# A two-layer graph kernel: guarded parts without SyncE's DMAs, gates ahead of the branch, layer two's weights in another order

## The chip, the cores and the metric

One core of a Trainium2 chip runs the whole kernel. TensorE (PE) multiplies, VectorE (DVE), ScalarE (ACT) and GpSimd (POOL) do the rest, SyncE (SP) issues most of the loads. The metric is the device time of one launch in microseconds (us); the lower, the better.

## The reference, cut to what matters

625 nodes with 512 features, 20,625 edges (10,000 in both directions and the loops), float32. Two layers. Layer 0, where the change lies, is a relational graph network of two inner layers, a linear attention, and a mixture of experts:

```python
def rgcn_gate_layer(x, row, col, edge_type, basis, att, gate_w, root, bias):
    w = jnp.einsum('rb,bio->rio', att, basis)          # 2 relations from 30 bases of 512 x 512
    x_j = x[col]
    msgs = [jax.nn.sigmoid(x_j @ gate_w[r, :, 0])[:, None] * x_j @ w[r] for r in range(2)]
    msg = jnp.where((edge_type == 0)[:, None], msgs[0], msgs[1])
    return jax.ops.segment_sum(msg, row, num_segments=625) + x @ root + bias

h = relu(rgcn_gate_layer(xn, ..., basis1, att1, gate_w1, root1, bias1))
gnn = rgcn_gate_layer(h, ..., basis2, att2, gate_w2, root2, bias2)
x = x + gnn + linear_attention(xn) @ W_out + b_out
x = x + one_of_8_experts(layernorm(x))
```

Layer 1 (a graph attention network, another attention, two of eight experts) fills the second half of the time and is not touched.

## The kernel before

The nodes are held as five tiles of 125. Nothing is gathered by edge: the kernel first counts, for each relation and each pair of nodes, the edges between them. One field of a float32 holds five nodes tiles and both relations in two bits each (`count_group`, `decode_fields`), ten tiles `counts` of 125 x 626. Messages are then a dense product of the counts with what each node sends. Should a pair have more edges than two bits hold, the fields are wrong; a sum over all of them, compared with the number of edges, gives a `flag`, and four guarded parts (`with tc.If(again > 0)`, L530, L580 twice, L806) do the exact work: `count_any` counts in a loop and stores the exact counts in DRAM (`cexact`, `cover`), `over` adds products to open PSUM banks, and the last one reloads counts. With these inputs the flag is 0, and every guarded part is skipped. Each engine that has something in a guarded part passes its branch, and where it has DMAs there, it has to keep their semaphores in step on the skipped way.

The weights `w` of each relation, a sum over 30 bases, are made while the data streams in. There are two ways to do it:
- a **P step** (`Bases.product`, L330) does it on TensorE for 32 of the 512 input rows in two steps, 15 bases each. Its load is four DMAs of 240 KB on SyncE's queue (`rows_of`, L321). After each second one ScalarE copies the result (L334), and GpSimd sends it to its rows of `wmix` with four DMAs (L337);
- a **D step** (`Bases.add`, L355) does it on VectorE for one basis and 384 of the 512 rows: two instructions of 128 x 1536, one for each relation. Its load is one DMA of 768 KB (`basis`, L342).

Layer one's weights are all made by P steps (`mix`), behind the counting. Layer two's need 8 P steps (rows 0 to 127) and 30 D steps (rows 128 to 511). `PLAN` gives their order, `second("DDP")` puts the next steps of the plan at a place in the program, and `load_next` asks for the next load after each. All loads of bases share a pool of three buffers; load n waits for the step that used its buffer last, and it is queued on SyncE behind load n-1 and whatever else stands before it (`root`, `root2`, `wout`: 1 MB each, through `load_w`).

TensorE, VectorE and SyncE run this part in the order in which the program states it (`manual_schedule`). That order is: the last counts are decoded; head sums of the attention (`key_value_sums`) with the last `mix` products between; the flag; the branch at L530; gates of layer one (`gate_sums`: products, a copy on ScalarE, a second product, a sigmoid in `gates_of`) with a P step between; the attention's values for five tiles (`mixed_values`) with two D steps and a P step; `messages(1)`: ten groups of 8 matmuls, each followed by a step or two of the plan; bias rows; the branch of `over`; then for each of five tiles the root product, transposes, 20 products with the counts (`summed`) and two D steps; own products of layer two (`own_pairs`, root and attention's output) with more D steps; all that is left of the plan; `messages(2)` (line L139, 80 matmuls), its branch, and layer two's sums. `five_banks` gives five PSUM banks for the tiles: two pairs and a single one, taken in order. Further on, `loops_added` (L789) adds up the counts for layer 1 on GpSimd behind the last guarded part, while the experts' products run.

Of the kernel before, what the change touches and what calls it, by code (L numbers as in the profile page):

```python
# [8 lines left out]
F32 = mybir.dt.float32  # L9
F32R = mybir.dt.float32r  # L10
# [9 lines left out]
P = 125  # L20
NT = 5
# [3 lines left out]
ODG = 11  # L25
NW = 626
NB = 30
PLAN = "PDDPDPDDPDPDDPDDPDP" + 19 * "D"
BGROUPS = (15, 15)
BROWS = 8  # L30
EXTRA = 4
# [6 lines left out]
def cols(t):  # L38
    return slice(t * P, (t + 1) * P)
# [7 lines left out]
def kernel(ctx: ExitStack, tc: tile.TileContext, A, out: bass.AP):  # L47
# [123 lines left out]
    def one_bank():  # L171
        return banks[1].tile([128, BANK], F32, name="ps1")
# [85 lines left out]
        return flag  # L258

    cexact = tc.dram_tile([2 * NT, P, NW], F32, name="cexact")  # L260
    cover = tc.dram_tile([2 * NT, P, NW], F32, name="cover")

    def count_any():

        held = [w8.tile([128, KD * D], F32, tag="w", name="whole") for _ in range(3)]
        whole = [held[i // 3][:P, NW * (i % 3):NW * (i % 3) + NW] for i in range(9)]
        whole.append(dec.tile([P, NW], F32, tag="vf", name="whole9"))
        for c in whole:  # L270
            nc.gpsimd.memset(c, 0.0)
        with tc.For_i(0, NE, 1) as c:
            some = dec.tile([P, 3], I32, name="some")
            for i, n in enumerate(("src", "dst", "edge_type_2")):
                nc.sync.dma_start(some[:, i:i + 1], A[n].rearrange("(p c) -> p c", p=P)[:, bass.ds(c, 1)])
            ends = dec.tile([P, 3 + NT], F32, name="some_f")
            nc.vector.tensor_copy(ends[:, 0:1], some[:, 0:1])
            nc.vector.tensor_scalar(ends[:, 2:3], some[:, 2:3], 0.0, None, op0=OP.not_equal)
            nc.vector.tensor_scalar(ends[:, 1:2], some[:, 2:3], 0.0, None, op0=OP.is_equal)
            for t in range(NT):  # L280
                nc.vector.tensor_scalar(ends[:, 3 + t:4 + t], some[:, 1:2], -float(t * P), None, op0=OP.add)
            os_ = [ohp.tile([P, NW], BF, name="os") for _ in range(2)]
            for r in range(2):
                nc.vector.tensor_scalar(os_[r], iota, ends[:, 0:1], ends[:, 1 + r:2 + r],
                                        op0=OP.is_equal, op1=OP.mult)
            for t in range(NT):
                od = ohp.tile([P, 128], BF, name="od", bufs=1)
                nc.vector.tensor_scalar(od, iota[:, :128], ends[:, 3 + t:4 + t], None, op0=OP.is_equal)
                for r in range(2):
                    cnt = whole[NT * r + t]  # L290
                    main = aps.tile([128, BANK], F32, name="main")
                    tail = aps.tile([128, NW - BANK], F32, name="tail")
                    nc.tensor.matmul(main, od, os_[r][:, :BANK], start=True, stop=True)
                    nc.tensor.matmul(tail, od, os_[r][:, BANK:], start=True, stop=True)
                    nc.vector.tensor_add(cnt[:, :BANK], cnt[:, :BANK], main[:P])
                    nc.vector.tensor_add(cnt[:, BANK:], cnt[:, BANK:], tail[:P])
        for i, c in enumerate(whole):
            nc.sync.dma_start(cexact[i], c)
            short = counts[i // NT][i % NT]
            nc.vector.tensor_copy(short, c)  # L300
            nc.vector.tensor_sub(c, c, short.bitcast(F32))
            nc.sync.dma_start(cover[i], c)

    class Bases:

# [162 lines left out]
    nc.scalar.dma_start(part, A["L0_mix_b_out"][None, :])  # L468
    nc.gpsimd.tensor_add(row, row, part)
    own3 = three_rows(row, "own3")  # L470
    first_bases = Bases(1, wpool)
    wm1 = first_bases.w
    steps = list(range(8 * KD))

    def mix(n=1):
        for q in steps[:n]:
            first_bases.product(q, first_bases.rows_of(q))
        del steps[:n]
# [18 lines left out]
            pieces.pop(0)()  # L497
    tot = decode_fields(main0, tail0)
    mix()
    for p in range(4):  # L500
        key_value_sums(kvb, kphi, v, p)
        mix(p % 2)
    assert not steps
    flag = not_counts(tot)

# [38 lines left out]
    in_order.__enter__()  # L544
    second_bases.w = wm2 = wpool2.tile([128, 2, KD * D], F32, name="wmix")

    def gate_sums(psg, layer, t):

        ps = one_bank()
        for k in range(KD):  # L550
            nc.tensor.matmul(ps[32 * k:32 * k + 32, :P], gwp[layer - 1][:, k, :], xnT[:, k, cols(t)],
                             start=True, stop=True)
        g = tmpA.tile([128, P], F32, name="gsum", bufs=2)
        nc.scalar.copy(g, ps[:, :P])
        return lambda: mm(psg[:P, 2 * t:2 * t + 2], [(g, strips)])

    def gates_of(psg):
        gate = tmpA.tile([P, NT, 2], F32, name="gate")
        nc.scalar.activation(gate.rearrange("p t r -> p (t r)"), psg[:P, :2 * NT], AF.Sigmoid)
        return gate  # L560

    def messages(layer, gate, wm, between=""):

        parts = [[pool.tile([P, NT, D], F32R, tag="a", name=f"z{layer}{r}{j}") for j in range(2)]
# [13 lines left out]
    def over(parts, open_banks):  # L578

        with tc.If(again > 0):  # L580
            for i in range(2 * NT):
                r, t = i // NT, i % NT
                for j, ps in enumerate(open_banks):
                    c = stage_pool.tile([128, D], F32, tag="stage", name="c")[:P, :P]
                    nc.sync.dma_start(c, cover[i][:, cols(j)])
                    cr = stage_pool.tile([128, D], F32R, tag="stage", name="cr")[:P, :P]
                    nc.vector.tensor_copy(cr, c)
                    for part in parts[r]:
                        nc.tensor.matmul(ps[:P], cr, part[:, t, :], start=False, stop=False)

    def summed(parts, t):
        return [(cnt[j][:, cols(t)], part[:, j, :]) for cnt, ps in zip(counts, parts)
# [5 lines left out]

    def five_banks():
        a, b, c = two_banks(), two_banks(), one_bank()  # L600
        return [a[:, :BANK], a[:, BANK:], b[:, :BANK], b[:, BANK:], c]

    psg = one_bank()
    waiting = None
    for t in range(NT):
        late = gate_sums(psg, 1, t)
        if waiting:
            waiting()
        waiting = late
    second("P")  # L610
    waiting()
    gate = gates_of(psg)
    attn = nodes_tile(act, "attn")
    waiting = None
    for t in range(NT):
        r = attn[:, t, :]
        z = small.tile([P, 8], F32, name="z")
        mixed_values(r, z, qT, kvb, t)
        if waiting:
            waiting()  # L620
        waiting = lambda r=r, t=t: transpose_rows(ps1, r, qT, t)
        second({0: "D", 2: "D", 4: "P"}.get(t, ""))
    waiting()
    attnT = qT
    root = load_w(A["L0_gnn_root1"], "root1")
    z = messages(1, gate, wm1, "D|P|D|DP|D|PD|D|PD|D|PD")
    second("P")
    root2 = load_w(A["L0_gnn_root2"], "root2")
    wout = load_w(A["L0_mix_W_out"], "wout")
    psg = one_bank()  # L630
# [5 lines left out]
    for t, ps in enumerate(banks5):  # L636
        dense(ps, [(xnT[:, k, cols(t)], root[:, k, :]) for k in range(KD)], False, False)
        if t:
            transpose_rows(ps1, xn[:, t - 1, :], xnT, t - 1)
        dense(ps, summed(z, t), False, True)  # L640
        nc.scalar.activation(xn[:, t, :], ps[:P], AF.Relu)  # L641
        if sums:
            sums.pop()()
        if t:
            sums.append(gate_sums(psg, 2, t - 1))
        second("DD")

    def own_pairs(t):
        return ([(xnT[:, k, cols(t)], root2[:, k, :]) for k in range(KD)]
# [4 lines left out]
        dense(ps, [(ones3, own3)], True, False)  # L654
    dense(banks5[0], own_pairs(0), False, False)
    transpose_rows(ps1, xn[:, 4, :], xnT, 4)
    second("DD")
    dense(banks5[1], own_pairs(1), False, False)
    sums.pop()()
    gate_sums(psg, 2, 4)()  # L660
    gate = gates_of(psg)
    for t in range(2, NT):
        second("DD")
        dense(banks5[t], own_pairs(t), False, False)
    second((len(plan) - sum(done.values())) * "D")


# [121 lines left out]
    def loops_added(behind):  # L789
# [16 lines left out]
            cnt.append(both)  # L806
        with tc.If(again > 0):
            for t in range(NT):
                nc.sync.dma_start(cnt[t], cexact[t])
                more = spare("more")  # L810
                nc.sync.dma_start(more, cexact[NT + t])
                nc.gpsimd.tensor_add(cnt[t], cnt[t], more)
        for t in range(NT):
            nc.gpsimd.tensor_add(cnt[t][:, cols(t)], cnt[t][:, cols(t)], ident[:P, :P])
# [701 lines left out]
```

## Time and profile before

| | us |
|---|---|
| median of 3 runs | 991.92 |
| lowest, highest | 988.98, 994.53 |
| profiled execution | 991.51 |
| its span | 989.7 |
| TensorE busy in the span | 903.4 |
| VectorE busy | 487.2 |

The stages, from the trace (us from the start of the span):

| stage | from, to | TensorE busy | VectorE busy | granted clock | DMA share |
|---|---|---|---|---|---|
| counting, attention's inputs, layer one's weights | 12, 167 | 142.94 | 102.90 | 0.97 | 0.87 |
| head sums, flag | 167, 176 | 7.90 | 6.74 | 1.00 | 0.91 |
| branch, gates, attention's values | 176, 206 | 18.34 | 10.70 | 0.77 | 0.47 |
| messages of layer one | 206, 266 | 54.67 | 38.47 | 0.97 | 0.79 |
| sums of layer one, own products of layer two | 266, 350 | 82.50 | 66.71 | 1.00 | 0.71 |
| messages and sums of layer two | 350, 412 | 61.07 | 16.62 | 1.00 | 0.18 |
| router and experts of layer 0 | 412, 600 | 170.88 | 73.37 | 0.95 | 0.55 |
| layer 1 | 600, 990 | 365.14 | 168.08 | 0.98 | 0.15 |

A line of a timeline gives start, duration, engine, source line, operation and tiles, and in brackets how long the engine had been idle and what released it. A line of waits gives engine, its instruction, what it waited for, the sum, the number of waits and the longest. PEld is TensorE's weight load; SPq, DVEq and the like are an engine's sequencer.

### The profile page before, as it was taken

To read this page: it belongs to the slowest core of one execution; us is meant where nothing else is said; L and a number is where in the kernel's file an instruction comes from. 1 tells how busy PE (TensorE), PEld (TensorE's weight loads), DVE (VectorE), ACT (ScalarE), POOL (GpSimd) and SP (SyncE) were. 2 spreads that over 40 slices of the span, in tenths; PEclk is the share of its full clock that TensorE was granted. 3 is DMA by queue.
4 is the path that set the end of the run, shared out by engine and by line. 5 is a ranking of instruction groups with operands and counts; after the bars stand their busy time and mean duration, and the time that the engine had idled before them with its cause. 6 is when DMAs were issued, how large, how long until landed. Compare 5 with 4: busy or idle time off the path is not lost.

```text
span 989.7 us, 10203 instructions
## 1 busy us (share of the span) xinstructions
PE 903.4 (91%) x3670; PEld 490.6 (50%) x3670; DVE 487.2 (49%) x966; ACT 239.6 (24%) x423; POOL 130.8 (13%) x199
## 2 busy tenths in 40 slices
PE   3699999689799999899987999999997999997997
PEld 1334445433266445786655455555553644444543
DVE  6956565357669812432224742222337663666320
ACT  0122114221011012201114623323234352311310
POOL 4522121101100110060020000000000000011410
PEclk9799999799999999989998999999999999997999
DMA  7898899577776750279872111121230204020001
GB/s 202 234 231 210 208 237 240 147 213 217 234 254 225 253 205 2 85 234 329 291 286 84 58 42 43 43 85 43 85 106 0 86 1 126 1 86 1 1 3 50
DMA packets 73895, 135.63 MB, mean 137 GB/s; under 512 B 10002, under 2 KB 12173, under 8 KB 73836
## 3 DMA queue, kind: packets, MB, share of 16 engines
q1 hardware_dynamic: 66456, 122.10, 40.3%
q0 software_dynamic: 6720, 11.50, 3.7%
q10 hardware_dynamic: 660, 1.29, 0.5%
q8 instruction: 32, 0.52, 0.2%
q14 instruction: 27, 0.22, 0.1%
HBM read 123.37 MB, written 8.85 MB: 134 GB/s over the span
## 4 chain that ended last, share of the span: by engine, by line
PE 37%; DVE 7%; issue 6%; DMA 2%; ACT 1%; POOL 1%; POOLq 0%; DVEq 0%; ACTq 0%
PE ps L139 20%; PE ps L134 12%; PE ps L1457 3%; DMA bb<-in_L_gnn_b_dram 1%; PE ps L1082 1%; DVE ln_st L105 1%; DMA yg<-yd,slot 1%; DVE y L1308 1%; DVE y L1283 0%; POOL x L1385 0%; POOL yd L974 0%; DVE gat_e L1033 0%; DVE ln_st L1312 0%; DMA wl<-in_L_gnn_W_dram 0%; DMA a_row<-in_L_gnn_a2d_dram 0%
## 5 line engine op out<-in xcount | busy, mean ns | idle before, releaser
L355 DVE SCALAR_TENSOR_TENSOR wmix<-basis,att,wmix 128x1536 f32<-128x1536 f32 x58 | 101.5, 1809 | 22.3 <-DMA basis<-in_L_gnn_basis_dram 21.7
L228 DVE TENSOR_SCALAR os<-iota,edges,wbits 125x626 bf16<-125x626 f16 x165 | 65.0, 468 | 40.9 <-PE tail L231 40.9
L134 PE MATMUL ps<-y1T,wh 128*128 128x512 f32 (+1 forms) x256 | 74.5, 440 | 1.4 <-DVE hm L1216 0.9
L230 PE MATMUL main<-os,odg 125*128 125x512 bf16 x165 | 52.7, 415 | 22.3 <-DVE os L228 22.2
L139 PE MATMUL ps<-hm,wh 128*128 128x512 f32 (+1 forms) x256 | 71.7, 433 | 0.0
L337 POOL DMA_DIRECT2D wmix<-stage x80 | 45.8, 575 | 186.3 <-ACT stage L334 184.7
L139 PE MATMUL ps<-wmix,xnT 128*125 128x512 f32 x160 | 70.1, 595 | 0.0
L134 PEld LDWEIGHTS ps<-y1T,wh 128*128 128x128 f32 x256 | 41.1, 190 | 33.7 <-issue 30.6
L139 PEld LDWEIGHTS ps<-hm,wh 128*128 128x128 f32 x256 | 39.7, 191 | 30.7 <-issue 30.7
L597 PE MATMUL ps<-z,counts 125*125 125x512 f32 x200 | 49.2, 400 | 0.9 <-DVE x L735 0.8
L139 PEld LDWEIGHTS ps<-wmix,xnT 128*125 128x125 f32 x160 | 29.7, 188 | 39.6 <-issue 36.6
L1226 DVE TENSOR_TENSOR acc<-acc,sg 128x625 f32<-128x625 f32 x15 | 12.2, 811 | 64.1 <-ACT sg L1224 64.1
L1216 DVE TENSOR_SCALAR hm<-ps,bh 128x625 f32<-128x625 f32 x32 | 27.7, 866 | 31.4 <-PE ps L134 31.4
L597 PEld LDWEIGHTS ps<-z,counts 125*125 125x125 f32 x200 | 36.4, 186 | 11.1 <-issue 1.4
L139 PEld LDWEIGHTS ps<-xgT,w1e 128*128 128x128 f32 x320 | 36.5, 192 | 8.1 <-ACT xgT L956 8.1
L139 PE MATMUL ps<-xgT,w1e 128*128 128x128 f32 x320 | 38.3, 278 | 1.5 <-ACT xgT L956 1.5
L573 DVE SCALAR_TENSOR_TENSOR z<-ps,gate,z 125x512 fp32r<-125x512 f32 x20 | 15.0, 749 | 48.2 <-ACT z L572 48.2
L1214 ACT ACTIVATE hm<-ps,bh 128x625 f32<-128x625 f32 x32 | 25.0, 782 | 55.3 <-PE ps L134 55.3
L330 PE MATMUL mix<-basis,att 120*32 120x512 f32 x256 | 37.0, 614 | 1.3 <-issue 1.1
L230 PEld LDWEIGHTS <-odg 125*128 125x128 bf16 x165 | 17.4, 105 | 41.9 <-DVE odg L224 16.8
L139 PE MATMUL ps<-w2e,hTe 128*128 128x512 f32 x80 | 37.5, 595 | 0.1
L597 PE MATMUL ps<-root,xnT 128*125 128x512 f32 x80 | 36.5, 599 | 1.1 <-ACT xn L641 0.9
(342 smaller groups left out, 1414.7 us busy)
## 6 DMA issues: line engine op xcount, KB each, us to landing
basis<-in_L_gnn_basis_dram SPq DMA_DIRECT2D x160, 240.0 KB
basis<-in_L_gnn_basis_dram SPq DMA_DIRECT2D x30, 768.0 KB
w1e<-in_L_ffn_W_dram SPq DMA_DIRECT2D x10, 1024.0 KB
w2e<-in_L_ffn_W_dram SPq DMA_DIRECT2D x10, 1024.0 KB
wh<-in_L_gnn_Wh_dram SPq DMA_DIRECT2D x4, 1024.0 KB
xd<-stage POOLq DMA_DIRECT2D x12, 256.0 KB, 4.0
wmix<-stage POOLq DMA_DIRECT2D x80, 32.0 KB, 4.8
b2row<-in_L_ffn_b_dram SPq DMA_DIRECT2D x10, 256.0 KB
```

Source lines behind the costliest of these rows:

```text
L134: nc.tensor.matmul(ps[:m, lo:hi], l, r[:, lo:hi], start=(i == 0), stop=(i == len(pairs) - 1))
L139: nc.tensor.matmul(ps, l, r, start=(i == 0), stop=(i == len(pairs) - 1))
L228: nc.vector.tensor_scalar(os_, iota, edges[:, 0, c:c + 1], wfield[:, c:c + 1], op0=OP.is_equal, op1=OP.mult)
L230: nc.tensor.matmul(main0, od[:, c - c0, :], os_[:, :BANK], start=c == 0, stop=c == NE - 1)
L330: nc.tensor.matmul(self.acc[32 * j:32 * j + 32, :], atts[self.layer][g][:k], bt[:k, j, :], start=(g == 0), stop=(g == 1))
L337: nc.gpsimd.dma_start(self.w[p0:p0 + 8, :, k * D:(k + 1) * D], sg[32 * j:32 * j + 16, :])
L355: nc.vector.scalar_tensor_tensor(w, bf, c, w, op0=OP.mult, op1=OP.add)
L573: nc.vector.scalar_tensor_tensor(lo[:, t, :], ps[:P], g, hi[:, t, :].bitcast(F32), op0=OP.mult, op1=OP.subtract)
L597: nc.tensor.matmul(ps[:P], l, r, start=first and i == 0, stop=last and i == len(pairs) - 1)
L1214: nc.scalar.activation(hm[:, m, :], ps[:, :N], AF.Relu, bias=b)
L1216: nc.vector.tensor_scalar(hm[:, m, :], ps[:, :N], b, 0.0, op0=OP.add, op1=OP.max)
L1457: nc.tensor.matmul(ps[:P], hs[:, e, cols(t)], w2[e // 4][:, e % 4, :], start=e == 0, stop=e == 7)
```

## The change

- Guarded parts: the DMAs in `count_any`'s end, in `over` and in `loops_added` are issued by GpSimd and no longer by SyncE. `count_any` stores the rounded counts too (`cshort`), so that `over` can load the rest straight into `counts` and restore them after.
- Gates of layer one: `gate_sums` runs between the head sums, ahead of the flag and the branch; the raw sums are kept in `raw`, and only the sigmoid stays behind the branch.
- Layer two's steps: `PLAN` begins with nine D's, then P's come singly; none stands in the gates' or the attention's stage but one D at its end; six D's stand in `messages(1)`, and P steps in the tiles of layer one's sums and layer two's own products.
- `five_banks` gives the banks in the order first half of the first pair, first half of the second, then the second halves.

```diff
-PLAN = "PDDPDPDDPDPDDPDDPDP" + 19 * "D"
+PLAN = "DDDDDDDDDPDDDPDDPDDDPDDDPDDPDDPDDPDD" + 2 * "D"
...
+    cshort = tc.dram_tile([2 * NT, P, NW], F32R, name="cshort")
...
-            nc.sync.dma_start(cexact[i], c)
+            nc.gpsimd.dma_start(cexact[i], c)
             short = counts[i // NT][i % NT]
             nc.vector.tensor_copy(short, c)
-            nc.vector.tensor_sub(c, c, short.bitcast(F32))
-            nc.sync.dma_start(cover[i], c)
+            nc.gpsimd.dma_start(cshort[i], short)
+            rest = dec.tile([P, NW], F32R, tag="part", name="rest", bufs=3)
+            nc.vector.tensor_sub(rest, c, short.bitcast(F32))
+            nc.gpsimd.dma_start(cover[i], rest)
...
+    psg = aps.tile([128, BANK], F32, tag="main", name="psg")
+    late = []
     for p in range(4):
         key_value_sums(kvb, kphi, v, p)
+        late.append(gate_sums(psg, 1, p))
+        if p:
+            late.pop(0)()
         mix(p % 2)
+    late.append(gate_sums(psg, 1, 4))
+    for f in late:
+        f()
+    raw = rowsA.tile([P, 2 * NT], F32, name="raw")
+    nc.vector.tensor_copy(raw, psg[:P, :2 * NT])
     assert not steps
     flag = not_counts(tot)
...
         with tc.If(again > 0):
             for i in range(2 * NT):
                 r, t = i // NT, i % NT
+                nc.gpsimd.dma_start(counts[r][t], cover[i])
                 for j, ps in enumerate(open_banks):
-                    c = stage_pool.tile([128, D], F32, tag="stage", name="c")[:P, :P]
-                    nc.sync.dma_start(c, cover[i][:, cols(j)])
-                    cr = stage_pool.tile([128, D], F32R, tag="stage", name="cr")[:P, :P]
-                    nc.vector.tensor_copy(cr, c)
                     for part in parts[r]:
-                        nc.tensor.matmul(ps[:P], cr, part[:, t, :], start=False, stop=False)
+                        nc.tensor.matmul(ps[:P], counts[r][t][:, cols(j)], part[:, t, :], start=False, stop=False)
+                nc.gpsimd.dma_start(counts[r][t], cshort[i])
...
-        return [a[:, :BANK], a[:, BANK:], b[:, :BANK], b[:, BANK:], c]
-
-    psg = one_bank()
-    waiting = None
-    for t in range(NT):
-        late = gate_sums(psg, 1, t)
-        if waiting:
-            waiting()
-        waiting = late
-    second("P")
-    waiting()
-    gate = gates_of(psg)
+        return [a[:, :BANK], b[:, :BANK], a[:, BANK:], b[:, BANK:], c]
+
+    gate = gates_of(raw)
...
-        second({0: "D", 2: "D", 4: "P"}.get(t, ""))
     waiting()
+    second("D")
...
-    z = messages(1, gate, wm1, "D|P|D|DP|D|PD|D|PD|D|PD")
-    second("P")
+    z = messages(1, gate, wm1, "D||D|D||D|D||D")
...
-        second("DD")
+        second(("DDP", "DDDP", "DDP", "DDDP", "DDD")[t])
...
-    second("DD")
+    second("PDDP")
     dense(banks5[1], own_pairs(1), False, False)
...
     for t in range(2, NT):
-        second("DD")
         dense(banks5[t], own_pairs(t), False, False)
+        second(("DDP", "DDP", "DD")[t - 2])
...
-                nc.sync.dma_start(cnt[t], cexact[t])
+                nc.gpsimd.dma_start(cnt[t], cexact[t])
                 more = spare("more")
-                nc.sync.dma_start(more, cexact[NT + t])
+                nc.gpsimd.dma_start(more, cexact[NT + t])
```

More of the change, by code (lines that the diff above doesn't have):

```diff
@@ L260 @@
     cexact = tc.dram_tile([2 * NT, P, NW], F32, name="cexact")
-    cover = tc.dram_tile([2 * NT, P, NW], F32, name="cover")
+    cshort = tc.dram_tile([2 * NT, P, NW], F32R, name="cshort")
+    cover = tc.dram_tile([2 * NT, P, NW], F32R, name="cover")
     def count_any():
@@ L470, with gate_sums, gates_of @@
     own3 = three_rows(row, "own3")
+    def gate_sums(psg, layer, t):
+        ps = one_bank()
+        for k in range(KD):
+            nc.tensor.matmul(ps[32 * k:32 * k + 32, :P], gwp[layer - 1][:, k, :], xnT[:, k, cols(t)],
+                             start=True, stop=True)
+        g = (ohp.tile([128, P], F32, tag="os", name="gsum") if layer == 1 else
+             tmpA.tile([128, P], F32, name="gsum", bufs=2))
+        nc.scalar.copy(g, ps[:, :P])
+        return lambda: mm(psg[:P, 2 * t:2 * t + 2], [(g, strips)])
+    def gates_of(psg):
+        gate = rowsA.tile([P, NT, 2], F32, name="gate")
+        nc.scalar.activation(gate.rearrange("p t r -> p (t r)"), psg[:P, :2 * NT], AF.Sigmoid)
+        return gate
     first_bases = Bases(1, wpool)
@@ L545 @@
     second_bases.w = wm2 = wpool2.tile([128, 2, KD * D], F32, name="wmix")
[L547 to L560, printed above, removed]
     def messages(layer, gate, wm, between=""):
```

## The prediction

> **What bounds the kernel now.** The page shows TensorE busy for 903.4 us of a span of 989.7 at a granted clock of 0.969. That mean says little about the stretch the change touches, from the end of the edge counts (about 173) to layer two's messages (350.39), so I read that stretch: first the page's groups, then waits, timelines and the table by stage.
>
> From the page's groups:
>
> ```profile
> L355 DVE SCALAR_TENSOR_TENSOR wmix<-basis,att,wmix 128x1536 f32<-128x1536 f32 x58 | 101.5, 1809 | 22.3 <-DMA basis<-in_L_gnn_basis_dram 21.7
> L330 PE MATMUL mix<-basis,att 120*32 120x512 f32 x256 | 37.0, 614 | 1.3 <-issue 1.1
> L337 POOL DMA_DIRECT2D wmix<-stage x80 | 45.8, 575 | 186.3 <-ACT stage L334 184.7
> ```
>
> A D step is two instructions of L355, 3.46 us back to back, and VectorE's only large idle time before them is a basis load. A P step is eight matmuls of L330, 1.06 us when its data is there.
>
> The timeline from 173 to 194, around the first guarded part:
>
> ```profile
> 176.13 0.15 DVE L257 TENSOR_SCALAR flag<-ps 1x1 int32<-1x1 f32 x1 [0.37 <-PE ps L255]
> 177.70 3.88 POOL L337 DMA_DIRECT2D wmix<-stage  x7 [1.26 <-DVEq L531]
> 183.79 0.43 ACT L554 COPY gsum<-ps 128x125 f32<-128x125 f32 x2 [7.13 <-SPq L531]
> 184.10 0.58 PE L139 MATMUL ps<-strips,gsum 128*125 128x2 f32 x2 [6.76 <-ACT gsum L554]
> 187.87 1.94 PE L330 MATMUL ps<-basis,att 120*32 120x512 f32 x8
> 192.14 0.17 DVE L385 TENSOR_SCALAR z<-ps 125x8 f32<-125x8 f32 x1 [15.87 <-PE ps L139]
> ```
>
> SyncE holds the branch until its loads in flight have landed; ScalarE's first copy waits for SyncE, TensorE for ScalarE (6.76). VectorE's first attention instruction comes at 192.14, and layer one's messages start at 205.43.
>
> The waits from 200 to 268, messages of layer one:
>
> ```profile
> PEld ps L330 <- DMA basis<-in_L_gnn_basis_dram: 17.9, 14, 4.6
> DVE wmix L355 <- DMA basis<-in_L_gnn_basis_dram: 13.6, 4, 5.8
> PE ps L330 <- DMA basis<-in_L_gnn_basis_dram: 5.2, 4, 3.7
> ```
>
> Here TensorE waits for P loads: the stage took 60.4 us (205.43 to 265.79) against 34.5 for the same 80 matmuls alone and 6 P steps at 1.06, so about 19.5 us of it is waiting. Then come VectorE's timeline from 284 and TensorE's from 340:
>
> ```profile
> 286.11 55.42 DVE L355 SCALAR_TENSOR_TENSOR wmix<-basis,att,wmix 128x1536 f32<-128x1536 f32 x32 [8.10 <-DMA basis<-in_L_gnn_basis_dram]
> ```
>
> ```profile
> 346.96 3.60 PE L597 MATMUL ps<-wout,qT 128*125 128x512 f32 x8
> 350.39 34.50 PE L139 MATMUL ps<-wmix,xnT 128*125 128x512 f32 x80
> 390.72 4.88 PE L597 MATMUL ps<-z,counts 125*125 125x512 f32 x20 [0.78 <-DVE x L735]
> ```
>
> VectorE's D steps end at 341.6, TensorE gets to the messages of layer two at 350.39: TensorE sets the time, with 9 us to spare on VectorE. The question of this change is whether that stays so.
>
> **The change, part by part.**
>
> 1. *Gates ahead of the branch.* In before, the gates and a P step fill 183.8 to 190.2, after the stall. In after, five gate groups stand between the head sums and the last mix product. Their copies queue on ScalarE behind the counts and a stage copy, free at about 175.6; one group took 1.09 from the next in before (184.61, 185.70, 186.79), so five end near 181.1, with the sums between them 181.4 to 182.4. The last mix product (1.06), the sum of the totals (0.19) and the flag (0.15, with 0.4 to 0.9 between) put the flag at 184.5, 8.2 later than 176.28. From flag to branch took 1.4 (176.28 to 177.70), so mixed values start at 185.9 against 190.18.
>
> 2. *Guarded DMAs on GpSimd.* SyncE's skip path no longer waits for the loads in flight. GpSimd's does, for its own: the last four of `L337`, issued at 183.3 to 185.5 (0.56 each), land 4.8 (page's median) to 5.7 (this stretch) later, about 190.7. A semaphore instruction of GpSimd follows that the trace of before does not have: I take 0.5, bounds 0 and 2 (VectorE's small rows are 0.15, a GpSimd DMA issue 0.56, the slowest branch row 1.4). Behind it on GpSimd stand only layer two's `wmix` DMAs, due 40 us later; but VectorE's first attention instruction waits for it too: 191.5 (191 to 193) against 192.14. From there to the messages took 13.3 in before, with two D steps on VectorE (2.0 and 3.53) or, by TensorE, stalls of 1.30 and 2.77 and a P step of 1.9. Without them 7.4 to 7.8 remain. So messages of layer one start at 199.3 (197.5 to 201), **6.1 earlier**.
>  At the second guarded part (before layer one's sums) GpSimd is long idle; nothing waits. At the third (layer two's sums) its clearing DMAs, issued after VectorE's last D for some 9 us plus 4 to land, are done before the 34.5 us of messages are: 0, with about 14 us of cover. At L807/L809 the indirect DMAs land (440.1) before GpSimd's additions end (442.3), so just the new instruction delays 442.50 POOL, then VectorE's `neg`, ScalarE's `xgT` and TensorE at 447.99, which already waits 0.54: **+0.5** (0 to 2). SyncE's own wait there (4.9) goes, but TensorE is continuous from 448 to 512: 0.
>
> 3. *Layer two's steps in another order.* This is the large term. TensorE alone, from messages of layer one to messages of layer two: 34.5 + 1.3 bias + 46.3 for the five summed tiles (3.45 + 0.37 + 4.75 + 0.55, about 9.3 each) + 1.2 + 34.4 own products (5 x 6.87) + 1.3 gates + 8.5 P steps = 127.5. If nothing waited, that is 199.3 + 127.5 = 327, 23 us sooner. But the stage must also load and add 30 D's. There are three basis buffers and one queue on SyncE, and a load is asked for when the step that held its buffer is done. Packets of the basis queue in before: a D load (768 KB) lands 4.0 after its issue when alone, and VectorE starts 0.65 after that; in a row they are served in 2.2 to 2.3, directly behind P parts in 2.60 to 3.07 (I take 2.75); a P load is four issues of 0.84 to 0.9, 1.08 of service per part; 1 MB of root or output weights 3.7. I followed every step with these, from three landed loads at the start (t = 0 is 199.3):
>  - Six D's pass behind the messages, and steps 7, 8 after: VectorE is free at t = 43.6. Load 9 (the first P) is asked for at 36.0, takes SyncE to 39.6 and lands by 43; `root2` and `wout` follow it, served to 50.5; load 10 stands behind them and is usable at 53.1. VectorE starves **9.5**.
>  - From there D's get only two buffers whenever TensorE has not yet reached a loaded P. A load takes 4.0 + 0.65 + 0.12 while one D runs 3.46, so 1.4 is missing each time; with P parts ahead in the queue 2.4 to 3.6; where a D buffer is freed by a late P, 6.3. In order: 1.4, 3.6, 2.4, 2.8, 2.8, 6.3, 2.4, 6.3.
>  - Sum: 43.6 + 21 D x 3.46 (72.7) + 37.5 starved = 153.8. TensorE's own waits for P steps (10.8, 2.0, 6.6) put it at 145.9, so VectorE is last.
>  Messages of layer two then start at 353.4, **+3.0** on 350.39. With service 2.2, 2.4 and 1.0 it is 347.7; with 2.5, 3.0 and 1.15 it is 358.2; the start at 197.5 or 201 moves it by 1.8. So -5 to +10. In before the same work had no such end because the last 16 D's ran with three buffers and no P between (55.42 for 32 instructions).
>
> 4. *A colder start of layer two's messages.* TensorE would stand idle for some 7 us before them. From the table by stage:
>
> ```profile
> 176.00:184.00 8.00, 0.72 (x18) 0.37 (x16) 0.15 (x1) 0.80 (x3) 4.32 (x8) 0.85 0.71 211
> 184.00:188.00 4.00, 3.90 (x36) 2.71 (x40) 0.00 (x0) 1.18 (x6) 0.00 (x0) 0.50 0.01 4
> 286.00:350.00 64.00, 63.34 (x226) 34.36 (x226) 56.07 (x36) 5.16 (x12) 7.53 (x14) 1.00 0.70 248
> ```
>
>  After 7 us with next to no matmul the granted clock (third from the right) was 0.50 for 4 us, against 1.00 in a full stretch; a P step there took 1.94 for 1.06. Four us at half clock lose 2, so **+1.5** (0 to 3).
>  The Trainium skill ("TensorE: Matmul & The Clock Gate", Part 1) says that one idle window of about 3.4 us halves the clock and one busy window restores it; by that the loss would be about 1.7 at messages of layer two, and the waits of 10.8 and 6.6 at P steps would each cost TensorE as much, where it has 8 us of room.
>
> 5. *Banks in another order.* The wait of 0.78 at 390.72 on VectorE reading the other half of a pair goes: **-0.8** (0 to -0.8). Those of 0.69 and 0.22 in layer one's sums lie where VectorE will be last: 0.
>
> Sum on the profiled execution (991.51 us, 1.81 of it outside the span; the median is 991.92): 991.51 + 3.0 + 1.5 + 0.5 - 0.8 = **995.7**. The 6.1 won at the branch is inside the 3.0: it is eaten, with TensorE's waits, by VectorE's starving. Own range of this case: -5 to +10 for the steps, 0 to 3, 0 to 2, -0.8 to 0, gives 986 to 1004.
>
> **The rivals.**
> - *VectorE is not starved enough to matter* (0.25). If loads keep three D's ahead, VectorE would be done near t = 116 and TensorE sets the end. For it: 32 instructions in a row without a wait in before, and a P buffer is freed as soon as TensorE comes. Against: that run had no P loads and no weights in the queue. Full effect 327 to 330, that is -20 to -23: 969 to 971; with half of the 37.5 starved, -16: 976; with four fifths of it, 984. It decides where starving drops by over 9.
> - *The queue is slower behind P parts than I took* (0.30 together with the upper half of my own case). At 2.8 for every D and 1.15 per P part the D's alone give +7, and at 3.2 +11: 1000 to 1004. For it: one D behind parts took 3.07, and the DMA share in the messages stage is already 0.79. It decides from about 2.9 on.
> - *The change does not do what it says at the branch* (0.05): GpSimd's DMAs and its added instruction take longer than SyncE's stall did, and the messages start no earlier than 205.4. Since VectorE's D's hang on that start, +6 more: 1002. Speaks against it: 190.7 needs only the row's 4.8 to 5.7.
>
> **How the numbers follow.** My own case has 0.40 outside of these, mostly within 0.5% of 991.92 (5 us, about what a measurement of this kernel can tell from no change), but its centre lies near the upper edge. Faster by more: the first rival and little else, 0.27. Slower by more: the other two and the upper part of mine, 0.40. Within: 0.33. The range leaves out the full effect of the first rival and the far end of the second: 974 to 1004.
>
> **What the profile after would show.** Right: the flag near 184.5, no wait of ScalarE on SyncE, messages of layer one near 199; waits of `DVE wmix L355` on basis loads summing to 30 to 40 between 240 and 350, the first about 9 near 243 behind the output weights; TensorE waiting before layer two's messages, its clock at 0.5 in their first microseconds. Wrong: D steps in an unbroken row, TensorE reaching those messages without a wait, or a first attention instruction later than 195.

## The result, and the profile after

The changed kernel took 1006.8 us (median of 4 runs, 1002.8 to 1008.82) against 993.21 for the kernel before (median of 4): a ratio of 1.0139 (95% interval 1.0092 to 1.0186). It is slower by 1.4%, clear of the noise. The forecast was 995.7 with a range of 974 to 1004; slower was its likeliest case (0.40), but the time lies 2.8 us outside the range. The profiled execution (1007.95, span 1006.1, granted clock 0.948) is compared with that of before (991.51, span 989.7, 0.969).

The page's group of the D steps, as in before:

```profile
L358 DVE SCALAR_TENSOR_TENSOR wmix<-basis,att,wmix 128x1536 f32<-128x1536 f32 x58 | 101.7, 1813 | 40.9 <-DMA basis<-in_L_gnn_basis_dram 40.9
```

The same work, with 40.9 us of waiting for bases instead of 21.7. VectorE's timeline (start, duration, and in brackets the idle time ahead) shows where:

```profile
239.03 7.00 DVE L358 SCALAR_TENSOR_TENSOR wmix<-basis,att,wmix 128x1536 f32<-128x1536 f32 x4
256.12 7.00 DVE L358 SCALAR_TENSOR_TENSOR wmix<-basis,att,wmix 128x1536 f32<-128x1536 f32 x4 [10.10 <-DMA basis<-in_L_gnn_basis_dram]
264.50 3.54 DVE L358 SCALAR_TENSOR_TENSOR wmix<-basis,att,wmix 128x1536 f32<-128x1536 f32 x2 [1.38 <-DMA basis<-in_L_gnn_basis_dram]
270.76 7.01 DVE L358 SCALAR_TENSOR_TENSOR wmix<-basis,att,wmix 128x1536 f32<-128x1536 f32 x4 [2.71 <-DMA basis<-in_L_gnn_basis_dram]
...
321.60 7.00 DVE L358 SCALAR_TENSOR_TENSOR wmix<-basis,att,wmix 128x1536 f32<-128x1536 f32 x4 [6.44 <-DMA basis<-in_L_gnn_basis_dram]
332.10 7.01 DVE L358 SCALAR_TENSOR_TENSOR wmix<-basis,att,wmix 128x1536 f32<-128x1536 f32 x4 [3.49 <-DMA basis<-in_L_gnn_basis_dram]
346.44 13.92 DVE L358 SCALAR_TENSOR_TENSOR wmix<-basis,att,wmix 128x1536 f32<-128x1536 f32 x8 [7.33 <-DMA basis<-in_L_gnn_basis_dram]
```

In before the last 32 of these instructions came in one row, ending at 341.5; now they come in twos, fours and sixes and a last eight, with a gap ahead of each, and end at 360.4. TensorE's timeline:

```profile
202.42 34.50 PE L139 MATMUL ps<-wmix,xnT 128*125 128x512 f32 x80
...
265.65 4.82 PE L333 MATMUL ps<-basis,att 120*32 120x512 f32 x8 [9.13 <-DMA basis<-in_L_gnn_basis_dram]
...
355.99 1.09 PE L139 MATMUL ps<-wmix,xnT 128*125 128x512 f32 x2 [1.37 <-DMA wmix<-stage]
358.69 5.83 PE L139 MATMUL ps<-wmix,xnT 128*125 128x512 f32 x9 [1.61 <-DVE wmix L358]
```

Messages of layer one run without a break, as meant (34.50 instead of 60.4 with the P steps between), and start 3 us sooner than in before (202.4, before 205.4). Messages of layer two start with two products at 355.99 and then wait for VectorE until 358.69: TensorE no longer sets the time. The third product needs only the first of the last D step's two instructions, so it starts 1.7 ahead of VectorE's end. The granted clock was 0.66 from 358 to 363 and 1.00 from there on.

The branch, from the timelines of GpSimd and VectorE around it:

```profile
186.18 2.23 POOL L340 DMA_DIRECT2D wmix<-stage  x4 [7.41 <-ACT gsum L482]
```

```profile
194.58 0.76 DVE L393 TENSOR_TENSOR attn<-ps,z 125x256 f32<-125x256 f32 x2 [3.73 <-DMA wmix<-stage]
```

SyncE's stall is gone, but VectorE now waits for GpSimd's transfers: 3.73 us at its first writing of attention's values. In the sequencer's records the last of these, issued at 187.9, had landed by 192.4; then an instruction that adds to the semaphores of GpSimd's queues takes 1.47 us, and VectorE's own waits on them another 0.6. That instruction at the first guarded part and at the last (duration in ns, then its start in us):

```profile
L560 POOLq INC_SWDGE_SEM  x1: 1467/1467/1467, 192.5 to 192.5; - x1
L809 POOLq INC_SWDGE_SEM  x1: 2153/2153/2153, 451.7 to 451.7; - x1
```

### The profile page after: what moved, and what is told of

It reads as the page before. It is cut to its first block, busy times and chain, and to the rows that moved or that the text cites. A ratio compares the mean times of both kernels' runs of the same rounds, so it can differ in the third digit from the quotient of the medians.

```text
span 1006.1 us, 10192 instructions
## 1 busy us (share of the span) xinstructions
PE 912.3 (91%) x3670; PEld 499.4 (50%) x3670; DVE 488.1 (49%) x967; ACT 239.6 (24%) x423; POOL 130.8 (13%) x199
## 4 chain that ended last, share of the span: by engine, by line
PE 47%; DVE 5%; DMA 4%; issue 2%; ACT 1%; POOL 1%; SPq 0%; POOLq 0%; DVEq 0%; ACTq 0%
PE ps L139 27%; PE ps L134 12%; PE ps L1459 3%; PE ps L609 2%; DMA xd<-xn,slot 2%; PE ps L1084 1%; DMA a3s<-in_L_gnn_a3s_dram 1%; DVE ln_st L105 1%; DVE y L1310 1%; DMA yg<-yd,slot 0%; DMA wl<-in_L_gnn_W_dram 0%; PE ps L126 0%; DVE ln_st L1314 0%; POOL yg L1023 0%; DMA a_row<-in_L_gnn_a2d_dram 0%
## 5 line engine op out<-in xcount | busy, mean ns | idle before, releaser
L358 DVE SCALAR_TENSOR_TENSOR wmix<-basis,att,wmix 128x1536 f32<-128x1536 f32 x58 | 101.7, 1813 | 40.9 <-DMA basis<-in_L_gnn_basis_dram 40.9
L1228 DVE TENSOR_TENSOR acc<-acc,sg 128x625 f32<-128x625 f32 x15 | 12.2, 811 | 64.1 <-ACT sg L1226 64.1
L609 PEld LDWEIGHTS ps<-z,counts 125*125 125x125 f32 x200 | 36.5, 186 | 10.2 <-issue 1.7
L230 PEld LDWEIGHTS <-odg 125*128 125x128 bf16 x165 | 17.4, 106 | 41.6 <-DVE odg L224 16.5
L231 PE MATMUL tail<-os,odg 125*128 125x114 bf16 x165 | 37.4, 226 | 0.0
```

The lines of the kernel that those rows point to most:

```text
L230: nc.tensor.matmul(main0, od[:, c - c0, :], os_[:, :BANK], start=c == 0, stop=c == NE - 1)
L231: nc.tensor.matmul(tail0, od[:, c - c0, :], os_[:, BANK:], start=c == 0, stop=c == NE - 1)
L358: nc.vector.scalar_tensor_tensor(w, bf, c, w, op0=OP.mult, op1=OP.add)
L609: nc.tensor.matmul(ps[:P], l, r, start=first and i == 0, stop=last and i == len(pairs) - 1)
```

## The experiments

Each kernel is told by its difference from the changed kernel ("after") or from before. Two marks are read from the timeline of each profile: the start of the first product of layer one's messages, and of the third of layer two's (the first that needs VectorE's D steps). The expectations read the same marks 0.2 to 0.3 sooner (202.2 for 202.4, 358.5 for 358.7). The column after them is the time from there to GpSimd's first addition behind the last guarded part. A mark is one execution's: after, e4 and e6 have the same code up to layer one's messages and reach them at 202.4, 203.2 and 200.4, so a difference of 2 between two kernels there says little. Each ratio is to runs of before that were taken with the experiment (medians of before 995.19 for e1 to e4, 996.05 for e5 to e8).

| kernel | messages one | messages two | from there to the last guard's end | ratio to before (95%) |
|---|---|---|---|---|
| before | 205.4 | 351.3 | 91.3 | 1 |
| after: order, gates, guards, banks | 202.4 | 358.7 | 95.3 | 1.0139 (1.0092, 1.0186) |
| e1: after, order of before | 206.3 | 359.5 | 92.4 | 1.0123 (1.0090, 1.0157) |
| e2: before, new order alone | 197.4 | 354.6 | 92.5 | 1.0035 (1.0013, 1.0057) |
| e3: before, guards alone | 204.4 | 360.8 | 94.2 | 1.0103 (1.0078, 1.0129) |
| e4: after, two weights later | 203.2 | 352.2 | 95.1 | 1.0052 (1.0031, 1.0072) |
| e5: after, guards on SyncE | 197.4 | 355.9 | 92.5 | 1.0035 (1.0002, 1.0068) |
| e6: after, quarter of the P loads | 200.4 | 339.9 | 93.7 | 1.0205 (1.0153, 1.0258), see below |
| e7: another order, banks | 197.4 | 332.8 | 90.5 | 0.9807 (0.9751, 0.9862) |
| e8: after, gates behind the branch | 198.5 | 353.6 | 95.5 | 1.0040 (1.0012, 1.0068) |

**e1, the order put back**; the rest as changed.

```diff
-PLAN = "DDDDDDDDDPDDDPDDPDDDPDDDPDDPDDPDDPDD" + 2 * "D"
+PLAN = "PDDPDPDDPDPDDPDDPDP" + 19 * "D"
...
+    second("P")
     gate = gates_of(raw)
...
-    z = messages(1, gate, wm1, "D||D|D||D|D||D")
+    z = messages(1, gate, wm1, "D|P|D|DP|D|PD|D|PD|D|PD")
+    second("P")
...
```

> The changed kernel with layer two's steps in the order and places of before (gates ahead, guards on GpSimd and the bank order stay). Theory (the order makes VectorE starve for bases, three buffers and one queue): VectorE's last D ends well before TensorE needs it again, its waits on basis loads fall from 41 us to below 20, messages of layer two start at 352 (350 to 354) instead of 358.7, and the time is 3 us above before (0 to +6): what GpSimd's waits cost stays. Rival (the gates and GpSimd's guards are what costs): messages of layer two stay at 357 or later and the time stays 12 us or more above before.

VectorE waits 18.3 and its D steps end at 338.8, as the theory had it, but messages of layer two start no sooner, and the time is 11.0 above before by the medians, 12.2 by the ratio: these are the rival's numbers. The waits of TensorE from 262 to 285 say why:

```profile
PE ps L609 <- DMA wmix<-stage: 7.7, 1, 7.7
```

In the old order a P step ends just ahead of the second guarded part, and GpSimd sends its result (issued 267.4 to 269.6). GpSimd's skip path then waits for that to land (277.0) and adds to its semaphores (1.76 us); TensorE's first products with the counts, which stand behind the guard, wait for both. So the old order is dear with guards on GpSimd, and the new one, whose P steps come behind that guard, is not: the parts of this change can't be priced one by one and summed.

**e2, the order alone**; gates, guards and banks as before.

```diff
-PLAN = "PDDPDPDDPDPDDPDDPDP" + 19 * "D"
+PLAN = "DDDDDDDDDPDDDPDDPDDDPDDDPDDPDDPDDPDD" + 2 * "D"
...
-    second("P")
     waiting()
     gate = gates_of(psg)
...
-        second({0: "D", 2: "D", 4: "P"}.get(t, ""))
     waiting()
+    second("D")
...
-    z = messages(1, gate, wm1, "D|P|D|DP|D|PD|D|PD|D|PD")
-    second("P")
+    z = messages(1, gate, wm1, "D||D|D||D|D||D")
...
```

> The kernel before with only the order and places of layer two's steps from the changed kernel; gates, guards and banks as before. Theory: VectorE starves 35 to 45 us, messages of layer two start at 355 to 360, time 5 to 11 us above before, and no loss at the last guarded part. Rival: the order costs only where the gates and the guards are moved too; then the time is within 3 us of before.

VectorE waits 41.5 in all, the first time 10.6, and messages of layer two start at 354.6: the theory's mechanism, a little below its numbers (+3.5 us by the ratio, interval 1.3 to 5.7, expected 5 to 11). The rival's bound on the time, 3, lies inside that interval; what speaks against it is the mark, 3.3 later than in before with neither gates nor guards moved. Messages of layer one start at 197.4, 8 sooner than before, without the gates moved: it is the two D's and two P's taken out of that stage that does it.

**e3, the guards alone**; gates, order and banks as before.

```diff
...
-            nc.sync.dma_start(cexact[i], c)
+            nc.gpsimd.dma_start(cexact[i], c)
...
+                nc.gpsimd.dma_start(counts[r][t], cover[i])
...
-                nc.sync.dma_start(cnt[t], cexact[t])
+                nc.gpsimd.dma_start(cnt[t], cexact[t])
...
```

> The kernel before with only the guarded DMAs moved to GpSimd. Theory: SyncE's stall at the first branch goes and ScalarE's first gate copy comes at about 178 instead of 183.8; GpSimd's wait for its wmix transfers and its semaphore instruction (1.5 to 2.2 us) take its place, done at about 187, so the first attention instruction comes at 187 to 189 instead of 192.1 and messages of layer two 3 to 5 us sooner; at the last guarded part GpSimd's additions come 2 to 2.7 later. Time 1 to 3 us below before. Rival: GpSimd's waits cost as much as SyncE's or more at the first branch; then the time is 2 us or more above before.

The theory missed and the rival's number held: 10 above before by the ratio. There is a reason at each guard. At the first, from the timeline:

```profile
183.84 0.43 ACT L557 COPY gsum<-ps 128x125 f32<-128x125 f32 x2 [6.53 <-DMA wmix<-stage]
183.95 3.88 POOL L340 DMA_DIRECT2D wmix<-stage  x7 [6.86 <-DMA wmix<-stage]
```

ScalarE's first copy stands at 183.84 as in before (183.79): it waits for GpSimd's semaphores now and not for SyncE's, and GpSimd's own remaining transfers, issued from 177.70 in before, wait too. At the second guard TensorE loses 6.2 us, for the same reason as the 7.7 in e1, and at the last GpSimd's additions come 2.9 later after layer two's messages than in before.

**e4, the two weights later.**

```diff
-    root2 = load_w(A["L0_gnn_root2"], "root2")
-    wout = load_w(A["L0_mix_W_out"], "wout")
...
         second(("DDP", "DDDP", "DDP", "DDDP", "DDD")[t])
+        if t == 1:
+            root2 = load_w(A["L0_gnn_root2"], "root2")
+        if t == 2:
+            wout = load_w(A["L0_mix_W_out"], "wout")
```

> The changed kernel with the loads of root2 and wout asked for behind the second and third of the five summed tiles, not ahead of the first. Theory (buffers and the queue as a whole): the first wait of VectorE falls from 10 to 2 or 3, but the weights then stand ahead of later loads; the waits sum to 38 or 39 instead of 41, messages of layer two come 1 to 2 us sooner than 358.7, time about 2 us below the changed kernel. Rival (the two weights ahead of one load are the cause): the sum falls by 8 and messages of layer two come at about 350.

Between the two, nearer the rival:

```profile
DVE wmix L358 <- DMA basis<-in_L_gnn_basis_dram: 33.7, 8, 6.7
```

VectorE's waits fall by 7.2, the first of them from 10.1 to 3.0, and messages of layer two come 6.4 sooner. The two weights ahead of load 10 cost 6 to 7 us, not 1 to 2; the other 34 stay without them.

**e5, the guards back on SyncE** (with the code of before inside them), gates, order and banks as changed.

```diff
...
-                nc.gpsimd.dma_start(counts[r][t], cover[i])
...
+                    nc.sync.dma_start(c, cover[i][:, cols(j)])
...
-                nc.gpsimd.dma_start(cnt[t], cexact[t])
+                nc.sync.dma_start(cnt[t], cexact[t])
...
```

> The changed kernel with the guarded DMAs back on SyncE (with the code they had there); gates, order and banks stay changed. What the runs so far say (GpSimd's guards cost: the wait for wmix and a semaphore instruction of 1.47 us at the first branch, 2.15 us at the last): the three D loads in flight at the branch were issued by 172 and have landed when the flag comes (186.6), so SyncE passes at once, the first attention product comes near 191 instead of 194.6, messages of layer one at 198.5 instead of 202.2, those of layer two at 355 instead of 358.5, and the last guarded part costs 2 less: time about 6 below the changed kernel, 7 to 9 above before. Rival (SyncE's own waits at the second and the last guarded part give it back): within 2 us of the changed kernel.

VectorE's first writing of attention's values, which waited 3.73 in after, comes 3.9 sooner:

```profile
190.70 0.76 DVE L390 TENSOR_TENSOR attn<-ps,z 125x256 f32<-125x256 f32 x2 [0.19 <-DVE z L386]
```

SyncE doesn't pass at once, as the expectation had it: the third of its loads was issued at 185.1, and its records show it at the branch until 190.4; but VectorE's first attention instruction, which waits for products, starts only at 190.1, so little of this is felt. Messages of layer one start 5.0 sooner than in after, more than was forecast. At the second guard SyncE waits for the loads ahead of it and issues its next basis load at 248.4 (243.6 in after); VectorE's first wait grows to 11.7, so 2.8 are left at layer two's messages, and 2.8 more come at the last guard. The time is 10 below the changed kernel by the two ratios, whose intervals are 7 and 9 wide, and 6.6 by the two profiles; 6 was forecast. At the last guard the two kernels differ in one line of GpSimd's timeline, after first, then e5:

```profile
453.97 2.71 POOL L816 TENSOR_TENSOR cnt<-cnt,ident 125x125 f32<-125x125 f32 x5 [2.71 <-DMA xd<-xn,slot]
```

```profile
448.41 2.72 POOL L815 TENSOR_TENSOR cnt<-cnt,ident 125x125 f32<-125x125 f32 x5 [0.18 <-POOLq L808]
```

The additions begin 2.71 us after the sums before them with GpSimd's guard, 0.18 with SyncE's; the indirect transfers had landed in both, and 2.15 of the 2.71 are the instruction that adds to the semaphores.

**e8, the gates back behind the branch**, guards on GpSimd, order and banks as changed.

```diff
-        late.append(gate_sums(psg, 1, p))
...
-    raw = rowsA.tile([P, 2 * NT], F32, name="raw")
-    nc.vector.tensor_copy(raw, psg[:P, :2 * NT])
...
-    gate = gates_of(raw)
+    for t in range(NT):
+        late = gate_sums(psg, 1, t)
+        ...
+    gate = gates_of(psg)
```

> The changed kernel with layer one's gates behind the branch again (without a P step between them); guards on GpSimd, order and banks stay changed. If the gates ahead of the branch cost (the flag came at 186.8 with them and at 176 to 177 without): messages of layer one start at 198 to 199 instead of 202.2, layer two's at 354 to 355 instead of 358.5, time about 4 below the changed kernel. If they gain what was forecast: messages of layer one at 204 or later, time 2 or more above the changed kernel.

Messages of layer one start 3.9 sooner than in after, those of layer two 5.1, as the first case had it; the time is 10 below the changed kernel by the two ratios, and 7.4 by the two profiles, of which 2.7 lie in layer 1 (see its point below). With e2 and e5 this makes a table of four for the start of messages of layer one: neither moved 197.4, gates ahead 197.4, guards on GpSimd 198.5, both 202.4 (200.4 to 203.2 over the three kernels with that code). Each alone costs nothing or 1; together they cost 3 to 6. ScalarE's first copy behind the branch says why, in e2 and then in e8:

```profile
183.51 0.43 ACT L554 COPY gsum<-ps 128x125 f32<-128x125 f32 x2 [5.37 <-SPq L531]
183.63 0.43 ACT L557 COPY gsum<-ps 128x125 f32<-128x125 f32 x2 [5.25 <-DMA wmix<-stage]
```

With the gates behind the branch, the wait is as long with GpSimd's guard as with SyncE's, and the gates follow it. With the gates ahead, the flag comes 9 later. By then SyncE's loads have landed, or land while the attention's first products run (e5), but GpSimd's last four transfers are issued only as the flag comes (186.2 to 187.9), and its wait stands behind the flag unhidden until 194.

**e6, a quarter of the P loads.**

```diff
-            for j in range(4):
+            for j in range(4 if self.layer == 1 else 1):
                 nc.sync.dma_start(bt[:BROWS * n, j, :], src[i0 + j, b0:b0 + n])
```

> The changed kernel with a quarter of each P load of layer two (one DMA of 240 KB, not four, its rows used for all four products): part of the computation is left out. Theory (what stands in the queue and in the three buffers makes VectorE starve): VectorE's waits on basis loads fall from 41 us to 22 to 28, layer two's messages start at 344 (340 to 348) instead of 358.5. Rival (the two weights ahead of one load are nearly all of it): the waits stay above 36 and the messages above 354.

```profile
DVE wmix L358 <- DMA basis<-in_L_gnn_basis_dram: 23.6, 15, 5.0
```

VectorE's waits fall to 23.6, and messages of layer two start at 339.9, a shade below the forecast's 340; 2 of the 18.8 were there at messages of layer one. Its whole time (1015.14) says nothing of the change: layer two's values are others, and the experts' first products (`xgT`, `w1e`) number 384 in it and 320 in before, from 418.4 to 525.0 (106.6 us) against 430.4 to 505.9 (75.5). Up to layer two's messages the same instructions run but for the loads left out, and there it is read.

**e7, an order found by the same reckoning.** Before's gates and guards, the banks as changed, and an order chosen by the step-by-step reckoning of the prediction, with the two weights asked for later:

```diff
+PLAN = "DDDDDDDPPDDPPDDDDDPDDPDDDDDDDPDDDPDDDD"
...
+    second("DD")
+    z = messages(1, gate, wm1, "DDD|D||D||P|PDD||P|P")
...
+        second(('D', 'DDDDPDD', 'PDD', '', 'DDD')[t])
+        if t == 1:
+            root2 = load_w(A["L0_gnn_root2"], "root2")
+        if t == 3:
+            wout = load_w(A["L0_mix_W_out"], "wout")
...
+    second("DDPDD")
...
+        second(('DP', 'D', 'D')[t - 2])
...
```

> Gates and guards as before, banks as changed, and an order of layer two's steps chosen by following each load through three buffers and one queue: P's in close pairs, D's two or three in a row behind them, the weights asked for behind the second and fourth summed tile. Theory: the same reckoning that gave 34 to 38 us of starving for the changed order (measured 41) gives 23 to 30 here, VectorE and TensorE end together, and layer two's messages start at 335 (330 to 343) against 351 before: time 8 to 20 below before. Rival (the queue cannot bring the bases faster in any order): 348 or later, time no better than 3 below before.

Faster than both: 974.24 us, 0.9807 of before. The waits from 200 to 335 (17.4, below the 23 to 30 that were forecast), then TensorE's timeline:

```profile
DVE wmix L355 <- DMA basis<-in_L_gnn_basis_dram: 17.4, 8, 3.5
```

```profile
240.32 1.29 PE L597 MATMUL ps<-bias,ones 65*125 65x512 bf16 x5
...
328.55 3.60 PE L597 MATMUL ps<-wout,qT 128*125 128x512 f32 x8
331.99 13.47 PE L139 MATMUL ps<-wmix,xnT 128*125 128x512 f32 x31
```

TensorE goes from its own products into layer two's messages without a wait: it sets the time again, 18.4 us sooner than in before. The same 30 D's and 8 P's, the same three buffers, the same queue. Part of this may be the place of the two weights, which e7 moves too (6.4 in e4); no run parts the two.

## Why the prediction was wrong, point by point

Against the profiled execution of before, forecast and measured:

| stretch | forecast | measured |
|---|---|---|
| to the third product of layer two's messages | +3.0 | +7.4 |
| those messages | +1.5 | +1.8 |
| from their end to GpSimd's first addition behind the last guard | -0.3 | +2.2 |
| from there to layer 1's head products | 0 | +0.5 |
| the rest of layer 1 | 0 | +4.5 |
| sum (span) | +4.2 | +16.4 |

- **The steps' order (step 3): the mechanism was right, the size nearly.** Forecast were nine waits of VectorE: 9.5, 1.4, 3.6, 2.4, 2.8, 2.8, 6.3, 2.4, 6.3, sum 37.5. The trace has nine, ahead of the same steps: 10.1, 1.4, 2.7, 3.4, 3.4, 2.6, 6.4, 3.5, 7.3, sum 40.9. From the start of messages of layer one to VectorE's last D that makes 157.9 where 153.8 was forecast. TensorE's third product came 1.7 ahead of that end, which the forecast did not count (nor do its 199.3 and 153.8 quite add up to its 353.4), so 1.3 of the miss is left to this step. e2 shows that the order alone makes VectorE last (+3.3 at layer two's messages; the +3.0 of the forecast was for the whole change), e6 that the P loads in the queue make a good part of it, e7 that the same reckoning finds an order without it. The rival in which VectorE is not starved fell; the rival of a slower queue came in part, with 40.9 for 37.5. What the prediction did not see is how much room another order leaves: e7 takes 24 us off the waits with the same buffers and the same queue.
- **The branch (steps 1 and 2): the step that failed.** The price of GpSimd's wait behind the flag was too low. Messages of layer one were to start at 199.3 (197.5 to 201); they started at 202.4. The flag was done at 186.8 and not at 184.5: from 176 to 184 the granted clock was 0.66, and a mix product there took 1.93, not 1.06. GpSimd's last transfers were issued from 186.2 and not from 183.3, and had landed at 192.4 and not at 190.7. The instruction behind them, unseen in before and taken at 0.5 with bounds 0 and 2, took 1.47. Attention's values were first written at 194.6, where the forecast's 191.5 for the row 0.5 ahead of it makes 192.0: 2.6 of the 3.1 are there. The forecast had the gates ahead of the branch as a gain; e8 shows that beside GpSimd's guard they lose 2 to 5 us, because GpSimd's wait then begins 9 later. Of the 6.1 that it expected, it rightly gave all but 0.6 to the steps taken out of the stage (e2: 8, with gates and guards unmoved).
- **The second guarded part: right for this order**, nothing waited there. e1 and e3 show a price of 6 to 8 us that the new order avoids; the prediction did not see this dependence.
- **The last guarded part: mis-sized, the same price again.** 2.7 us of idle time at GpSimd, where before had 0.18 and 0.5 (0 to 2) more was put down; the bound from small rows of other engines did not hold for an instruction of that kind (2.15 us).
- **The colder start: right in size.** 1.8 measured for 1.5, with a clock of 0.66 from 358 to 363. TensorE stood idle for 1.37 and 1.61 us, 3.0 in all, not the 7 of the forecast. The Trainium skill ("TensorE: Matmul & The Clock Gate", Part 1) gives half a clock after an idle window of about 3.4 us. The trace agrees on the half (0.50 from 358.9 to 362.3); but in the 3.4 us ahead of it TensorE had 1.28 us of products, so here the window need not be idle throughout.
- **The banks: right but small.** The wait of 0.78 on `x` is gone; a wait of 0.40 at TensorE's branch of the guard is there instead, so half of the 0.8 came.
- **The rest of layer 1: put at nothing, and +4.5 between the two profiles.** It is the same code, and took 408.6 instead of 404.1. Product by product, 4.0 of the 4.5 arise in three stretches in which after ran at a granted clock of 0.50 and before did not: 761.6 to 765.1 (+1.6), 768.5 to 771.9 (+0.6) and 908.4 to 911.8 (+1.8). The table by stretch around the first two, in after and then for the same products in before (the clock is the third figure from the right):

```profile
758.23:761.64 3.41, 1.02 (x7) 0.84 (x7) 3.25 (x7) 2.30 (x4) 0.00 (x0) 1.00 0.00 0
761.64:765.05 3.41, 3.11 (x4) 0.67 (x2) 2.22 (x6) 0.82 (x1) 0.00 (x0) 0.50 0.00 0
765.05:768.46 3.41, 1.47 (x7) 1.02 (x8) 3.32 (x9) 1.44 (x3) 0.00 (x0) 1.00 0.01 2
768.46:771.88 3.42, 3.42 (x9) 1.88 (x8) 3.12 (x8) 1.48 (x3) 0.00 (x0) 0.50 0.00 0
```

```profile
746.29:749.70 3.41, 1.13 (x7) 0.89 (x8) 3.25 (x6) 2.06 (x4) 0.00 (x0) 1.00 0.00 0
749.70:753.11 3.41, 1.40 (x4) 0.32 (x2) 3.41 (x9) 1.17 (x2) 0.00 (x0) 1.00 0.00 0
```

In each of the ten traces all changes of the granted clock lie whole multiples of 3.413 us apart, as on a grid, and where that grid lies against the program differs from trace to trace. The time of layer 1 goes with it:

| kernels | first point of the grid after the first head product, us | time at 0.50 that before did not have | rest of layer 1 |
|---|---|---|---|
| before, e7 | 2.19, 2.18 | 0 | 404.1, 404.3 |
| e6, e8 | 0.47, 0.47 | 3.4 | 406.2, 405.9 |
| e2, e3 | 1.74, 1.74 | 6.8 | 407.0, 407.5 |
| e5 | 3.00 | 10.2 | 408.1 |
| after, e1, e4 | 0.28, 0.23, 0.44 | 10.2 | 408.6, 408.9, 408.9 |

So nearly all of the 4.5 is the clock, and these traces tie it to the place of the grid, not to the change: the profile of before, from which the forecast was reckoned, happened to have none of it. What sets the place of the grid stays open, and so does what makes the clock fall: it fell after a stretch with 1.02 us of products and held after one with 1.13, but also fell after one with 1.92 (905.0 to 908.4).

Two terms were mis-sized on one side, and both are the price of GpSimd's guard: the branch (+3.1) and the last guarded part (2.5 where 0.5 was forecast). The steps' term was 1.3 low and the messages' 0.3. The +4.5 of layer 1 comes on top by luck: without it the profiled execution would have taken 1003.5, just inside the range. How much of it the other executions had is not known, as they left no trace.

## What to carry to other kernels

Where an engine is fed through a few buffers and one queue, follow every load through them by hand: buffer free, issue, place in the queue, landing. Here that gave nine waits within about 1 us each, told that the order costs more than it frees, and found a better order that the same kernel had room for. What a wait costs depends on the work that another part of the change puts ahead of it or behind it; price parts together, at each place where they meet. And a guarded part that is never entered isn't free: in these runs whichever engine held its DMAs, SyncE or GpSimd, waited on the way past for all that it had in flight, and others with it (TensorE 6.8 us in before, 3.1 to 7.7 with GpSimd's guards). Last, look at the clock of code that was not touched before its time is put down to a change.

## What the runs showed of the hardware

- The instruction by which GpSimd adds to the semaphores of its DMA queues took 1.33 to 1.47 us at the first branch, 1.44 or 1.76 (e1 and e3) at the second guard, and 2.05 to 2.15 later on. It was expected at 0.5.
- The granted clock fell to 0.50 for 3.41 us though TensorE was not idle in the 3.41 us ahead (1.02 us of products ahead of 761.6 and 1.47 ahead of 768.5, in after), and before passed the same products at 1.00. Each stretch of this kind in layer 1 goes with 1.3 to 2.1 us more.
- In the packets of the basis queue of after (from 200 to 356, given to the loads in the queue's order, from the first packet of a load to the end of its last), a D load behind another D was served in 2.2 to 3.7 us, one in 4.5, directly behind P parts in 2.5 to 3.5, a P part in 0.9 to 2.0, and 1 MB in 2.9 to 4.1. The spread of one kind is larger than the difference that the prediction made between kinds (2.3 and 2.75).
